# Two layers of masked cross-attention on one core: maxima of the scores taken from ScalarE's copies in SBUF instead of from PSUM

## The chip, the cores and the metric

The kernel runs on one NeuronCore of a Trainium2 chip. The metric is the device time of one execution in microseconds (us): 3316.82, the median of three runs (3314.22 to 3318.01). All data is 32-bit floating point. TensorE multiplies matrices from SBUF into PSUM; VectorE, ScalarE and GpSimd work on elements; the sequencer of SyncE (SP) issues most DMAs. GpSimd is called POOL in the profile, VectorE DVE, ScalarE ACT, TensorE PE.

## The reference

Two attention layers follow one another on x (4 batches, 512 rows, 320 columns) with one context (4 batches, 1024 tokens of 512). Both have 20 heads of 16 columns. Cut to what matters:

```python
# layer 0: text = tokens 0..1019, ip = the last 4
q, k_t, v_t = x @ W_q, text @ W_k, text @ W_v              # split into heads
probs_t = softmax(q k_t^T / 4)                              # 1020 tokens
text_out = probs_t v_t
qsem = l2norm(probs_t @ text)                               # 512 columns per head and row
fused = q k_ip^T / 4 + 0.5 * qsem l2norm(ip)^T
ip_out = (softmax(fused) * spatial_mask) v_ip
x = (text_out + ip_out) @ W_out + b_out + x
# layer 1: text = tokens 0..76, ip = the other 947
out = softmax(q k^T / 4) v + softmax(q k_ip^T / 4) v_ip     # two softmaxes, own maxima
x = out @ Wo^T + bo + x
```

The product `probs_t @ text` (each head's probabilities with all 512 context columns) is the bulk of the arithmetic.

## The kernel before

**Passes.** A turn is 128 rows of one batch (16 turns); it has five groups of four heads, so there are 80 passes (`gi`), one for each turn and group. Scores lie with the tokens on partitions: a fill (`fill`, L547) computes, for four heads and half of the 1024 tokens, 16 products of 128 tokens by 128 rows into two PSUM tiles `sc` (two heads each, 1024 columns). ScalarE copies each into SBUF (`e`, 128 x 1024). Maxima over the tokens go the way that matters here: in `fill`, VectorE reduces each PSUM tile over its four token tiles into `m` (a half is `c`; for layer 0 the two halves are joined by `m<-m`); then a transpose of 32x32 blocks and a reduce to `zz` (`fold0`, L941), a transpose of `zz` on TensorE (`turn_tops`, L572, tile `mx`), a reduce to `zt` (`spread`, L578), a DMA to DRAM and one back as a broadcast, `bc`. `do_exp` then adds `bc` (minus the maximum) to `e` on VectorE and takes the exponent on ScalarE, in place; for the half `c == 0` GpSimd also subtracts one head's block from another (L964).

**Units.** A pass is two units of two heads (`Unit`, L1002). A unit multiplies exponents with the context by seven block products in place of eight (Strassen's scheme), 8 matmul records each: `part0` has products 11 and 21 of blocks, `part1` t1 and t2, `part2` 22 and t3, `part3` t4. They accumulate in three PSUM banks b1, b2, b3. GpSimd forms sums of exponents for them: `sum2` (tile `s`, L1032), L1051 and L1053. ScalarE copies the first product as `p1` and a later state of b1 as `u`; the state of b3 after t1 is copied by VectorE as `p5`, whose last 21 columns (the window that carries the values) have `p1` subtracted at once (L1064 and L1065). VectorE adds pairs of these (tile `c`) and ScalarE squares the sums; the 21 columns go to `pv`.

**Order.** `mm` (L77) keeps TensorE's instructions in program order, and `vec` (L90) does so for VectorE. ScalarE's and GpSimd's instructions are ordered by the tile framework's planner, which goes by its own costs; at run time every engine works through its queue in order. After each part, `stop(gi, k)` (L1262, k = 0 to 7 over the two units) issues other work: layer 0's next fill at k = 0 (first half) and k = 2 (second half), layer 1's fill at k = 4 and 6 (`visit`, L1241), its adds and exponents (`do_adds`), the exponents of the next pass (queue `ew`, one item at k = 1, one inside `part2` of the first unit, two at k = 6), projections of the next batch (queue `proj`), and what ends a turn (`after`, `late`, `norm`). `fold0` comes at k = 3. `part0` of the second unit and `part2` of the first issue the transposes of `zz` behind their products, and then what `between` returns: `ask`, the reduce to `zt` with the DMAs.

**Layer 1's two maxima.** In layer 1 tokens 0 to 76 and the others have separate maxima. The first token tile holds both, so the reduce of the first half leaves it out (`lo`), and `mask` (L626) joins it later as (e + cut) max m, where `cut[:, 1:2]` holds -1e30 on the first 77 partitions and 0 elsewhere; `x` is the copy with the opposite mask (L620).

`p1`, `p5`, `m` and `x` have one buffer each; `e` has eight for layer 0 and six for layer 1.

Of the kernel before, what the change touches and what calls it, by code (L numbers as in the profile page):

```python
# [15 lines left out]
ALU = mybir.AluOpType  # L16
AX = mybir.AxisListType
# [3 lines left out]
P = 128  # L21
# [24 lines left out]
EH = E // 2  # L46
WIN = EH + V0W
TH = TT // 2
# [8 lines left out]
def xattn_pair(ctx_stack: ExitStack, tc: tile.TileContext, a: dict, out: bass.AP):  # L57
    nc = tc.nc
# [18 lines left out]
    def mm(out, lhsT, rhs, start, stop, on=False):  # L77
        tc.keep_in_program_order(nc.tensor.matmul(out, lhsT=lhsT, rhs=rhs, start=start, stop=stop, skip_group_check=on))  # L78
# [11 lines left out]
    vec = InOrder(nc.vector)  # L90
# [46 lines left out]
    mask = cst.tile([P, TT + 1], F32, name="mask")  # L137
    last = cst.tile([P, 2], F32, name="last")
    cut = cst.tile([P, 2], F32, name="cut")
# [384 lines left out]
    after = deque()  # L524
    ew = deque()
    bits = deque()

    def gap(n=1):
        for _ in range(n):
            if bits:  # L530
                bits.popleft()()
# [15 lines left out]
    def fill(l, k, c, m, pl, tag, name):  # L547

        ps = [ps_sc.tile([P, 2, 512], F32, tag="sc", name=f"sc{name}_{c}_{i}") for i in range(2)]
        n = D + 1 - l  # L550
        for j in range(TH):
            t = (TH * c + j) * P
            for r in range(4):
                mm(ps[r // 2][:, r % 2, j * P : (j + 1) * P], kq[l][k][32 * r : 32 * r + n, t : t + P],
                   qq[l][k][32 * r : 32 * r + n, :], True, True)
        e = [pl.tile([P, 2, TH, P], F32, tag=tag, name=f"e{name}_{c}_{i}") for i in range(2)]


        lo = l * (1 - c)
        for i in range(2):  # L560
            nc.scalar.copy(e[i].rearrange("p h t s -> p (h t s)"), ps[i].rearrange("p h n -> p (h n)"))  # L561
            j = 1 - i
            vec.tensor_reduce(m[:, c, 2 * j : 2 * j + 2, :],
                              ps[j][:, :, lo * P : TH * P].rearrange("p h (t s) -> p h s t", s=P), AX.X, ALU.max)
        if c and not l:
            vec.tensor_tensor(m[:, 0], m[:, 0], m[:, 1], ALU.max)
        return e
# [10 lines left out]
    def spread(pt, rows, tag, name):  # L578

        n = rows * P // ZW  # L580
        zt = st2.tile([ZW, ZW], F32, tag="zt", name=f"zt{name}")
        vec.tensor_reduce(zt[:n, :], pt[:n, 0:P].rearrange("r (b j) -> r j b", j=ZW), AX.X, ALU.max, negate=True)
        zd = dr.tile([rows, P], F32, tag=tag, name=f"{tag}{name}")
        nc.sync.dma_start(zd.rearrange("h (k j) -> (h k) j", j=ZW), zt[:n, :])
        return zd
# [15 lines left out]
    def load_values(z, turn, g):  # L601
        v = st2.tile([P, TT + 1, V1Q], F32, tag="v1q", name=f"v1q_{turn}_{g}")
        nc.sync.dma_start(v, z.v1d[:, :, g * 4 * V1W : g * 4 * V1W + V1Q])
        return v

    class Once:
# [6 lines left out]
        def fill(self, c):  # L613
# [8 lines left out]
            if c:  # L622
                free.append(self.k)
                load_next()

        def mask(self):  # L626

            for i in range(2):
                x = self.m[:, 0, 2 * i : 2 * i + 2, :]
                vec.scalar_tensor_tensor(x, self.e[0][i][:, :, 0, :], cut[:, 1:2], x, ALU.add, ALU.max)  # L630

        def top(self, k):

# [25 lines left out]
        def ask(self, pt):  # L659

            zd = spread(pt, 8, "zd1", self.name)
            self.bc = bc = big.tile([P, 2, 4, P], F32, tag="bc1", name=f"bc{self.name}")
            keep(nc.sync.dma_start(bc[:NTXT1, 0], zd[0:4, :].partition_broadcast(NTXT1)))
            keep(nc.sync.dma_start(bc[NTXT1:, 0], zd[4:8, :].partition_broadcast(P - NTXT1)))
            keep(nc.sync.dma_start(bc[:, 1], zd[4:8, :].partition_broadcast(P)))
            self.v = load_values(self.z, self.turn, self.g)
# [22 lines left out]
    now = {"fill": None, "fold": None, "add": []}  # L689

    def load_next():
        if waiting and free:
            q = waiting.popleft()
            q.load(free.popleft())
            loaded.append((q, stops[0]))

    def begin(*where):
        now["fill"] = loaded.popleft()[0] if loaded and stops[0] >= loaded[0][1] + 2 else None
        if now["fill"]:
            now["fill"].where = where  # L700

    def do_fill(c):
        if now["fill"]:
            now["fill"].fill(c)

    def do_mask():
        if now["fill"]:
            now["fill"].mask()

    def do_fold(all=False):  # L710
        q = now["fill"]
# [6 lines left out]
    def do_rest():  # L718
        if now["fold"]:
            now["fold"].fold_rest()  # L720
# [281 lines left out]
    class Unit:  # L1002
# [43 lines left out]
        def part0(self, between):  # L1046
            self.b1, self.b2 = self.psum(0)[:, 0:WIN], self.psum(1)[:, 0:WIN]
            self.product(self.b1, "11", "11", True)
            self.p1 = big.tile([P, WIN], F32, tag="p1", name=f"p1_{self.name}")
            nc.scalar.copy(self.p1, self.b1)  # L1050
            nc.gpsimd.tensor_tensor(self.e("11"), self.e("11"), self.s2, ALU.add)  # L1051
            self.product(self.b2, "12", "21", True)
            nc.gpsimd.tensor_tensor(self.e("12"), self.e("12"), self.s2, ALU.subtract)  # L1053
            ask = between and between()
            self.add_square(self.b2[:, 0:EH], self.p1[:, 0:EH], 0, 0)
            vec.tensor_tensor(self.values(0), self.b2[:, EH:], self.p1[:, EH:], ALU.add)
            if ask:
                ask()

        def part1(self):  # L1060
            self.b3 = self.psum(2)[:, 0:WIN]
            self.product(self.b3, "11", "t1", True)
            self.p5 = big.tile([P, WIN], F32, tag="p5", name=f"p5_{self.name}")
            vec.tensor_copy(self.p5[:, 0:EH], self.b3[:, 0:EH])  # L1064
            vec.tensor_tensor(self.p5[:, EH:], self.b3[:, EH:], self.p1[:, EH:], ALU.subtract)  # L1065
            self.product(self.b1[:, 0:EH], "s2", "t2", False)
            self.u = big.tile([P, EH], F32, tag="u", name=f"u_{self.name}")
            nc.scalar.copy(self.u, self.b1[:, 0:EH])

        def part2(self, between):  # L1070
            self.product(self.b3[:, 0:EH], "12", "22", False)
            ask = between and between()
            self.add_square(self.b3[:, 0:EH], self.u, 0, 1)
            if ask:
                ask()
            if not self.i:
                item(ew)
            self.product(self.b1[:, 0:EH], "21", "t3", False)
            self.add_square(self.b1[:, 0:EH], self.p5[:, 0:EH], 1, 1)

        def part3(self):
            self.product(self.b1, "22", "t4", False)
            self.square(self.b1[:, 0:EH], 1, 0)
            vec.tensor_tensor(self.values(1), self.b1[:, EH:], self.p5[:, EH:], ALU.add)

    def finish(turn):
# [137 lines left out]
    for g in range(HG):  # L1224
        for r in range(4):
            c = 64 * g + D * r
# [8 lines left out]
    def item(*queues):  # L1235
        for q in queues:
            if q:
                q.popleft()()
                break

    def visit(gi, k):  # L1241

        if gi == len(G) - 1:
            if k == 0:
                begin(ep, "e0")
            if k == 4:
                begin(e1p, "e1")
            if k == 6:
                do_values()
                do_adds(2)  # L1250
            do_fill(k // 2 % 2)
            return
        if k < 4:
            fill0(gi + 1, k // 2)
        if k == 4:
            begin(e1p, "e1")
            do_fill(0)
        if k == 6:
            do_values()
            do_fill(1)  # L1260

    def stop(gi, k):  # L1262

        end = gi == len(G) - 1
        if k == 1:
            do_mask() if end else do_rest()
            item(ew)
        if k == 3:
            do_fold(True) if end else fold0(gi + 1)
        if k == 6:  # L1270
            item(ew)
            item(ew)
        if k == 7 and not end:
            do_fold(gi + 1 == len(G) - 1)
        if k == 7 and end and now["fill"]:
            now["fold"] = now["fill"]
            now["fill"] = None
            bits.extend(now["fold"].pieces())
        if k < 3:
            item(after, late, *([proj] if k else []))  # L1280
        elif k % 2:
            item(late, proj)
        do_adds(({3: 4, 7: 2} if end else {3: 1, 5: 3}).get(k, 0))
        if k == 3:
            item(norm)
        if k == 5:
            do_mask()
        if k % 2 == 0:
            visit(gi, k)
        stops[0] += 1  # L1290

    units = {}
# [7 lines left out]
    for gi, (turn, g) in enumerate(G):  # L1300
        b, s = TURNS[turn]
# [7 lines left out]
        for i in range(2):  # L1309
            u = units.pop((gi, i))  # L1310
            end = gi == len(G) - 1
# [20 lines left out]
    while late:  # L1332
        if now["fold"] and not bits:
            ask = do_maxima()
# [4 lines left out]
    ask = do_maxima()  # L1339
# [36 lines left out]
```

## Time and profile before

| | |
|---|---|
| median of three runs | 3316.82 us |
| profiled execution | 3314.02 us, of which the span of instructions is 3312.3 us |
| mean granted TensorE clock | 0.985 |
| busy: PE / PEld / DVE / ACT / POOL | 3208.6 / 2594.7 / 2506.2 / 1855.7 / 1043.7 us |
| VectorE's reduces of `sc` (620) | 706.9 us |
| VectorE's adds of `bc` to `e` (770) | 803.5 us |
| ScalarE's copies of `sc` (620) | 614.5 us |
| VectorE's copies of `p5` (160) | 66.7 us |

Busy time is the union of the instructions of an engine. A group's line in the profile shows count, busy time, mean duration of one in ns, the idle time of the engine just before them, and what ended it. A matmul in 32-bit precision stands as two records. Since an add has two tile names on the right (`e<-e,bc`), a step can be found by its tiles although helpers give it one line, L88.

### The profile page before, as it was taken

The numbers are of one execution on the slowest core, as the hardware profiler recorded it, in microseconds if no ns is written. First come the engines' busy times: TensorE is split into PE (matmuls) and PEld (weight loads), VectorE is DVE, ScalarE is ACT, GpSimd is POOL, SyncE is SP. The second block draws the span as 40 slices with busy tenths as digits, with TensorE's granted clock in tenths as the row PEclk, the third lists the DMA queues.
The fourth block names the chain that finished last, engine by engine and source line by source line (L and its number), as shares of the span: only waits on it lengthen the run. The fifth ranks groups of instructions, "written<-read, shape, count | busy, mean of one in ns | idle before, by whom it ended". The sixth has DMA issues, their size and how long they took to land.

```text
span 3312.3 us, 72573 instructions
## 1 busy us (share of the span) xinstructions
PE 3208.6 (97%) x27740; PEld 2594.7 (78%) x27740; DVE 2506.2 (76%) x4172; ACT 1855.7 (56%) x3373; POOL 1043.7 (32%) x1123
## 2 busy tenths in 40 slices
PE   7999999999999999999999999999999999999988
PEld 5777888878788788887878888887787778787765
DVE  3344577788877777778887787778898888889874
ACT  1333455566555555566655555566666656666643
POOL 3333223323332332323333232323333333333320
PEclk9999999999999999999999999999999999999987
DMA  6433344333444344332344434333233233232221
GB/s 213 112 79 97 96 117 96 92 71 65 102 99 125 92 119 118 75 79 65 68 101 127 121 90 109 97 72 70 58 86 89 63 67 69 59 72 62 64 54 39
DMA packets 648147, 293.89 MB, mean 89 GB/s; under 512 B 491530, under 2 KB 602282, under 8 KB 647802
## 3 DMA queue, kind: packets, MB, share of 16 engines
q1 hardware_dynamic: 646762, 285.65, 36.1%
q8 instruction: 221, 3.62, 0.5%
q0 software_dynamic: 864, 3.41, 0.4%
q14 instruction: 124, 1.02, 0.1%
q10 hardware_dynamic: 176, 0.20, 0.0%
HBM read 248.43 MB, written 40.47 MB: 87 GB/s over the span
## 4 chain that ended last, share of the span: by engine, by line
PE 80%; DVE 10%; DMA 5%; ACT 3%; issue 2%; SPq 1%; POOL 0%; DVEq 0%; POOLq 0%; ACTq 0%
PE b L78 52%; PE sc L78 9%; PE pt_v L78 4%; PE pv L78 4%; PE pt_k L78 4%; DVE e L88 4%; DMA bc<-zd 2%; PE pt_q L78 2%; DVE m L88 2%; PE pt_y L78 2%; DMA zd<-zt 1%; ACT e L561 1%; ACT e L675 1%; DVE x L88 1%; PE mx L78 1%
## 5 line engine op out<-in xcount | busy, mean ns | idle before, releaser
L88 DVE TENSOR_REDUCE m<-sc 128x256 f32<-128x1024 f32 (+1 forms) x620 | 706.9, 1156 | 240.9 <-PE sc L78 166.7
L88 DVE TENSOR_TENSOR e<-e,bc 128x1024 f32<-128x1024 f32 (+2 forms) x770 | 803.5, 1082 | 21.6 <-DMA bc<-zd 21.1
L78 PE MATMUL b<-xv_t,e 128*128 128x277 f32 x2560 | 686.2, 410 | 7.9 <-DVE c L88 7.8
L561 ACT COPY e<-sc 128x1024 f32<-128x1024 f32 x620 | 614.5, 1006 | 82.8 <-DVE m L88 34.2
L78 PE MATMUL b<-xv,e 128*128 128x277 f32 x2560 | 631.3, 398 | 9.2 <-ACT e L962 9.2
L78 PEld LDWEIGHTS b<-xv,e 128*128 128x128 f32 x2560 | 483.4, 190 | 130.6 <-ACT e L962 11.4
L964 POOL TENSOR_TENSOR e<-e 128x512 f32<-128x512 f32 x160 | 230.6, 1441 | 1114.0 <-ACT e L962 1114.0
L78 PEld LDWEIGHTS b<-xv_t,e 128*128 128x128 f32 x2560 | 460.7, 190 | 134.8 <-DVE c L88 11.8
L962 ACT ACTIVATE e<-e 128x1024 f32<-128x1024 f32 x320 | 338.5, 1058 | 225.4 <-DVE e L88 224.6
L675 ACT ACTIVATE e<-e 128x1024 f32<-128x1024 f32 x300 | 316.1, 1058 | 194.3 <-DVE e L88 185.8
L78 PEld LDWEIGHTS sc<-qq,kq 17*128 17x128 f32 (+1 forms) x9920 | 307.1, 186 | 89.9 <-issue 85.0
L78 PE MATMUL sc<-qq,kq 17*128 17x128 f32 (+1 forms) x9920 | 366.8, 283 | 2.1 <-DMA kq<-kd 1.5
L1036 ACT ACTIVATE junk<-c 128x256 f32<-128x256 f32 x480 | 197.6, 412 | 287.8 <-DVE c L88 281.0
L78 PE MATMUL b<-xs,e 128*128 128x256 f32 x1280 | 313.5, 389 | 36.2 <-DVE p L88 27.5
L1051 POOL TENSOR_TENSOR e<-e,s 128x512 f32<-128x512 f32 x160 | 208.4, 1302 | 420.1 <-PE b L78 419.4
L78 PE MATMUL b<-xs_t,e 128*128 128x256 f32 x1280 | 307.3, 384 | 0.0
L78 PEld LDWEIGHTS b<-xs,e 128*128 128x128 f32 x1280 | 241.6, 193 | 81.1 <-issue 47.1
L78 PE MATMUL b<-xs_t,s 128*128 128x256 f32 x1280 | 302.3, 379 | 0.0
L88 DVE TENSOR_TENSOR c<-b,p 128x256 f32<-128x256 f32 x320 | 132.9, 415 | 222.7 <-PE b L78 166.2
L78 PEld LDWEIGHTS b<-xs_t,s 128*128 128x128 f32 x1280 | 242.7, 190 | 39.6
L78 PEld LDWEIGHTS b<-xs_t,e 128*128 128x128 f32 x1280 | 241.8, 194 | 36.9 <-issue 1.0
L1032 POOL TENSOR_TENSOR s<-e,e 128x512 f32<-128x512 f32 x160 | 203.1, 1270 | 122.6 <-ACT e L962 101.5
(213 smaller groups left out, 3439.3 us busy)
## 6 DMA issues: line engine op xcount, KB each, us to landing
kq<-kd SPq DMA_DIRECT2D x632, 64.0 KB
bc<-zd SPq DMA_DIRECT2D x155, 256.0 KB
v1q<-v1d SPq DMA_DIRECT2D x80, 373.5 KB
xv<-v0d SPq DMA_DIRECT2D x320, 42.0 KB
xv_t<-v0d SPq DMA_DIRECT2D x320, 42.0 KB
bc<-zd SPq DMA_DIRECT2D x75, 154.0 KB
L_xattn_W_k<-in_L_xattn_W_k_dram SPq DMA_DIRECT2D x13, 640.0 KB
L_xattn_Wv_ip<-in_L_xattn_Wv_ip_dram SPq DMA_DIRECT2D x13, 640.0 KB
```

The source lines that it names most:

```text
L78: tc.keep_in_program_order(nc.tensor.matmul(out, lhsT=lhsT, rhs=rhs, start=start, stop=stop, skip_group_check=on))
L88: return lambda *args, **kw: keep(getattr(self.engine, name)(*args, **kw))
L561: nc.scalar.copy(e[i].rearrange("p h t s -> p (h t s)"), ps[i].rearrange("p h n -> p (h n)"))
L675: nc.scalar.activation(flat, flat, AF.Exp)
L962: nc.scalar.activation(flat, flat, AF.Exp)
L964: nc.gpsimd.tensor_tensor(e[:, 1], e[:, 1], e[:, 0], ALU.subtract)
L1032: nc.gpsimd.tensor_tensor(self.s2, self.e("21"), self.e("22"), ALU.add)
L1036: nc.scalar.activation(junk, x, AF.Square, accum_out=self.w["ss"][:, self.h + r, k : k + 1])
L1051: nc.gpsimd.tensor_tensor(self.e("11"), self.e("11"), self.s2, ALU.add)
```

## The change

Four things change.

- In `fill` the reduces from PSUM are gone. Behind ScalarE's two copies VectorE takes pairwise maxima of the copies: two steps of 512 columns for the first half of layer 0; four of 512 for every second half, which take in `m` twice; for the first half of layer 1 two masked steps of 256 columns ((e0 + cut) max e1) and two plain ones (e2 max e3). `mask` and its calls go.
- `p5` is copied whole (277 columns) by ScalarE; the subtraction of `p1` from its last 21 columns moves into `part3`, from SBUF to SBUF.
- A queue `mid` is emptied inside `fill`, between the copies and the maxima (or after `visit`, where no fill took place). Into it go `part0`'s first sums (`first_sums`), the `ew` item of the first unit's `part2`, and the second of the two at k = 6.
- In `part0`, `ask` is issued before the first sums instead of behind them.

```diff
+    mid = deque()
...
         e = [pl.tile([P, 2, TH, P], F32, tag=tag, name=f"e{name}_{c}_{i}") for i in range(2)]
-        lo = l * (1 - c)
         for i in range(2):
             nc.scalar.copy(e[i].rearrange("p h t s -> p (h t s)"), ps[i].rearrange("p h n -> p (h n)"))
-            j = 1 - i
-            vec.tensor_reduce(m[:, c, 2 * j : 2 * j + 2, :],
-                              ps[j][:, :, lo * P : TH * P].rearrange("p h (t s) -> p h s t", s=P), AX.X, ALU.max)
+        while mid:
+            mid.popleft()()
+        for i in range(2):
+            top, tiles = m[:, :, 2 * i : 2 * i + 2, :], e[i].rearrange("p h t s -> p t h s")
+            if c:
+                vec.tensor_tensor(top, top, tiles[:, 0:2], ALU.max)
+                vec.tensor_tensor(top, top, tiles[:, 2:4], ALU.max)
+            elif l:
+                vec.scalar_tensor_tensor(top[:, 0], tiles[:, 0], cut[:, 1:2], tiles[:, 1], ALU.add, ALU.max)
+                vec.tensor_tensor(top[:, 1], tiles[:, 2], tiles[:, 3], ALU.max)
+            else:
+                vec.tensor_tensor(top, tiles[:, 0:2], tiles[:, 2:4], ALU.max)
         if c and not l:
             vec.tensor_tensor(m[:, 0], m[:, 0], m[:, 1], ALU.max)
...
-        def mask(self):
-            for i in range(2):
-                x = self.m[:, 0, 2 * i : 2 * i + 2, :]
-                vec.scalar_tensor_tensor(x, self.e[0][i][:, :, 0, :], cut[:, 1:2], x, ALU.add, ALU.max)
...
             ask = between and between()
+            if ask:
+                ask()
+            mid.append(self.first_sums)
+
+        def first_sums(self):
             self.add_square(self.b2[:, 0:EH], self.p1[:, 0:EH], 0, 0)
             vec.tensor_tensor(self.values(0), self.b2[:, EH:], self.p1[:, EH:], ALU.add)
-            if ask:
-                ask()
...
             self.p5 = big.tile([P, WIN], F32, tag="p5", name=f"p5_{self.name}")
-            vec.tensor_copy(self.p5[:, 0:EH], self.b3[:, 0:EH])
-            vec.tensor_tensor(self.p5[:, EH:], self.b3[:, EH:], self.p1[:, EH:], ALU.subtract)
+            nc.scalar.copy(self.p5, self.b3)
...
-            if not self.i:
-                item(ew)
+            if not self.i and ew:
+                mid.append(ew.popleft())
...
             self.square(self.b1[:, 0:EH], 1, 0)
+            vec.tensor_tensor(self.p5[:, EH:], self.p5[:, EH:], self.p1[:, EH:], ALU.subtract)
             vec.tensor_tensor(self.values(1), self.b1[:, EH:], self.p5[:, EH:], ALU.add)
...
         if k == 1:
-            do_mask() if end else do_rest()
+            do_rest()
             item(ew)
...
         if k == 6:
             item(ew)
-            item(ew)
+            if ew:
+                mid.append(ew.popleft())
...
-        if k == 5:
-            do_mask()
         if k % 2 == 0:
             visit(gi, k)
+            while mid:
+                mid.popleft()()
```

More of the change, by code (lines that the diff above doesn't have):

```diff
@@ L704, in do_fill @@
             now["fill"].fill(c)
-    def do_mask():
-        if now["fill"]:
-            now["fill"].mask()
     def do_fold(all=False):
```

## The prediction

> **What bounds the kernel now.** I read the page's busy line first, then busy time in stretches of 100 us, then TensorE's waits, then the timeline of one pass, and last the groups by shape for prices.
>
> ```profile
> PE 3208.6 (97%) x27740; PEld 2594.7 (78%) x27740; DVE 2506.2 (76%) x4172; ACT 1855.7 (56%) x3373; POOL 1043.7 (32%) x1123
> ```
>
> TensorE is busy 97% of the span. In the stretches (length, busy PE, PEld, DVE, ACT, POOL, granted clock, DMA share, GB/s) there are two kinds:
>
> ```profile
> 1000.00:1100.00 100.00, 99.77 (x802) 80.79 (x801) 74.83 (x125) 58.95 (x103) 29.56 (x38) 1.00 0.48 125
> ...
> 2600.00:2700.00 100.00, 98.09 (x845) 79.37 (x844) 89.21 (x151) 60.96 (x111) 36.87 (x34) 0.98 0.31 67
> ```
>
> Where projections of the next batch are interleaved (the first), TensorE is full and VectorE has a quarter to spare; where there are none (the second: about 700 to 900, 1500 to 1700, 2300 to 2500, 2500 to 3150 us; "tight" below) VectorE is busy too. TensorE's waits between 100 and 3150 us:
>
> ```profile
> PE b L78 <- DVE p L88: 23.4, 19, 2.3
> PE b L78 <- issue: 8.7, 3, 2.9
> PE b L78 <- DVE c L88: 7.8, 14, 0.6
> PE b L78 <- ACT e L962: 6.4, 3, 2.7
> ```
>
> The columns are total us, times, longest. TensorE is idle 49.3 us of these 3050, so this is nearly all that can be won there, and 23.4 of it ends with VectorE's copy of p5 (the 8.7 "issue" stand at the same place: three ends of a turn). A gap of 1.9 us or more is followed some 11 us later by 3.4 us at half clock in most cases, which costs 1.7 us more. What could be lost shows in the timeline of a tight pass (start, us, engine, line, operation):
>
> ```profile
> 2898.71 1.17 PE L78 MATMUL sc<-qq,kq 17*128 17x128 f32 x32
> ...
> 2900.02 1.27 POOL L1032 TENSOR_TENSOR s<-e,e 128x512 f32<-128x512 f32 x1
> 2900.03 2.41 DVE L88 TENSOR_REDUCE m<-sc 128x256 f32<-128x1024 f32 x2 [0.79 <-PE sc L78]
> ...
> 2900.19 0.99 ACT L561 COPY e<-sc 128x1024 f32<-128x1024 f32 x1
> ...
> 2901.34 1.01 ACT L561 COPY e<-sc 128x1024 f32<-128x1024 f32 x1 [0.16 <-POOL s L1032]
> ...
> 2902.47 0.69 DVE L88 TENSOR_TENSOR m<-m 128x512 f32<-128x512 f32 x1
> ...
> 2903.19 0.71 DVE L88 STREAM_TRANSPOSE m<-m 128x512 f32<-128x512 f32 x1
> ...
> 2903.94 0.69 DVE L88 TENSOR_REDUCE zz<-m 128x16 f32<-128x512 f32 x1
> ...
> 2905.53 0.27 PE L93 MATMUL mx<-ident,zz 128*128 128x128 f32 x1
> ```
>
> After the second half of a fill (sc, ends 2899.88) VectorE reduces, joins the halves (m<-m), transposes, reduces to zz, ends 2904.63; TensorE comes to the transpose of zz (mx) at 2905.53. So the chain takes 4.75 us and TensorE allows 5.65. I measured this interval for all 80 passes: the chain takes 4.7 in nearly all; TensorE allows 5.65 in 30, 6.09 in 11, 7.3 or more in the rest, apart from the first pass.
>
> Prices (busy us, mean ns):
>
> ```profile
> L88 DVE TENSOR_REDUCE m<-sc 128x256 f32<-128x1024 f32 x470 | 564.2, 1222 | 206.8 <-PE sc L78 150.8 <-ACT e L561 52.5
> ...
> L88 DVE TENSOR_TENSOR x<-m 128x512 f32<-128x512 f32 x75 | 73.1, 974 | 2.5
> ...
> L88 DVE TENSOR_TENSOR m<-m 128x512 f32<-128x512 f32 x80 | 55.4, 692 | 2.7
> ```
>
> ```profile
> L1032 POOL TENSOR_TENSOR s<-e,e 128x512 f32<-128x512 f32 x160 | 203.1, 1270 | 122.6 <-ACT e L962 101.5 <-PE sc L78 11.6 <-ACT junk L1036 0.4
> ```
>
> **The change part by part.** The profiled execution took 3314.0 us, 2.8 below the median of 3316.8; the sum starts from 3314.0.
>
> *Busy time of VectorE.* Gone: 470 reduces of 1024 columns (564 us), 150 of 768 (143), 150 mask steps (66), the p5 copies (67). Added: 780 steps of 512 columns at 691 ns (539), 150 masked and 150 plain steps of 256 columns at 0.48 and 0.41 (134). That is 167 us less. It is worth time only where TensorE waits for VectorE.
>
> *The chain from sc to zz.* This sets my forecast. A step of 512 took 691 to 693 ns whenever GpSimd was not running an add (the m<-m row). After the change: ScalarE starts its first copy 0.12 us after sc and takes 1.0; the first maximum starts at 1.20. Four steps of 0.69, two of which read what the step before wrote (such pairs stood 0.03 apart, independent ones overlapped by 0.08), end at 3.94; m<-m at 4.66; from its end to the end of zz took 1.47, and the subtraction of p5's 21 columns, now queued there, adds 0.09: 6.22. mx then starts at about 6.28 instead of 5.65. Price: 0.63 us in 30 passes and 0.19 in 11, 21 us. Behind the waiting maxima on VectorE stand m<-m, the transpose, zz and then layer 1's adds; mx waits for zz, and ScalarE's next exponents for the adds. The exponent's add put in front (1.22 us) starts before sc ends and is over by 0.6, so it is covered by the copy; were it late, it would add up to 1.2.
>
> *GpSimd in that chain.* The reduces read PSUM: 319 of the 470 large ones overlapped a GpSimd add and took 1223 ns, the others 1217. Steps with two SBUF inputs don't: x<-m took 692 alone and 1421 where it overlapped one, and its row's mean of 974 is this mixture; GpSimd's adds go from 1.27 to 2.0. The exponent's ScalarE step, if ScalarE takes steps as the program issues them, now follows both copies (0.12 + 2.0 + 1.06 = 3.2 us after sc), and GpSimd's sum s (L1032) waits for just this; today it runs in the reduces' shadow. So it asks for the port amid the maxima (1.2 to 4.66). Does it get in between? At 1543.41 an add on GpSimd asked while VectorE ran a row of such adds; it ended 1.47 later, so after the running one, and VectorE's next add took 1.89 instead of 1.22. So I charge 1.27 less the 0.1 by which starts overlap, 1.15: the wait at mx becomes 1.78 us in 30 passes and 1.34 in 11, together 68 us. Without any collision it is 21; 68 is the likelier end, by that row.
>
> [...]
>
> *p5 on ScalarE.* 160 copies of 277 columns at 0.39 us (L1050's row). In the first half of a pass ScalarE has only the two copies of sc and a square in front: they end about 2.6 us after sc, p5 at 3.0, and TensorE needs it at 3.6: free. In the second half (layer 1's fill) two masked copies x of 0.51 and the squares stand there as well. Today ScalarE starts the copies of sc 0.9 to 1.0 late in tight passes, because an exponent waits for VectorE; 0.9 + 2.0 + 1.0 + 0.4 = 4.3 against 3.55. I charge 0.75 in 30 passes, 22 us; the bounds are 0 (p5 planned ahead of the x) and 1.7 (VectorE's adds come 0.9 later, behind the longer chain). This takes the place of 8 us of today's p5 waits outside ends of turns.
>
> *Ends of turns.* Nine tight ones hold 22.5 us of waits. There ScalarE's copies stand behind an exponent that waits for a row of small VectorE steps. p5 would come 0.4 earlier (two copies and 0.39 against reduces, 0.41 and 0.17), but layer 1's maxima, at the end of the same queue, can make that row up to 1.8 later. I take 0, bounds -4 and +16.
>
> *First sums behind the fill, the ask before them.* The sums (0.42 and 0.17) fill the wait for the first copy; their squares on ScalarE are in the p5 sum above. The ask's DMAs on SP's queue go out 0.6 earlier, and no wait for them binds today: 0. p1 stays in use until the subtraction, so the next unit's p1 copy starts up to 1 us later; the product that needs its bank comes more than 3 us after, so 0, and about 1 a pass if that cover goes. Moving the exponent's add behind the third sum frees that sum: the 7.8 us of "DVE c" go.
>
> *Later GpSimd adds, exponents, clock.* Block 11's add (L1051) must be ready at the first product after the fill; by the same collisions it comes 1.0 later and has 1.5 to spare (2922.72 against 2924.21): 0, bound 20. Three batch ends with "ACT e" may lose 2 each. Waits of 1.78 lie just below the 1.9 that half clock followed; bound 50 if they pass it.
>
> Sum: 68 + 22 - 8 - 8 = 74. 3314 + 74 = 3388; with the 2.8 by which the median lies above the profiled execution, 3391.
>
> **The rivals.** *Collision rarely binds* (GpSimd's sum comes before or after the maxima): 21 + 22 - 16 = 27, less where p5 goes first: 3323 to 3355. For it: s may be planned elsewhere; against: any moment in a stretch of 3.4 us collides.
>
> *Faster.* VectorE's relief decides: the waits for p5 (23.4 + 8.7), for c (7.8) and half of some 17 us of half clock go, 48 us, and the chain costs nothing: 3266, or up to 3307 where half of it is lost at mx. For it: VectorE is what TensorE waits for today, and loses 167 us of 2506. Against: these waits are latency at two places. It decides from the point where zz ends within 5.6 us of sc.
>
> *No difference.* The chain costs 21 and the p5 and c waits saved pay for it (32 + 8, of which half at ends of turns stays): 3310 to 3323.
>
> **How the numbers follow.** Chances: forecast 0.52 (3355 to 3440), collision rarely binds 0.25, no difference 0.08, faster 0.15. The range leaves out most of the faster case and the upper bounds of p5, the clock and GpSimd together: 3308 to 3440. About 0.2% (6.6 us) is what a measurement of this kernel can tell from no change: faster 0.15, same 0.07, slower 0.78.
>
> **What would show it.** Right: a wait "PE mx <- DVE zz" of 0.6 to 1.8 us, some 40 times, where there are three now; sc to zz at 6.2 to 7.4 us; steps m<-e with a mean well above 691; "PE b <- ACT p" in second halves; VectorE's busy time below 2506 but less so than by 167. Wrong: no wait at mx, or zz within 5.7 us of sc; a p5 that never binds; maxima at 691 on average, which would mean that GpSimd stays out of the way.

## The result: 3716 us, 12% slower

The changed kernel took 3716.12 us (median of five, 3710.87 to 3723.04) against 3316.82 before: a ratio of 1.120, 95% interval 1.118 to 1.122. The direction was forecast, the size was not: 400 us in place of 74. The profiled execution took 3720.5 us, span 3718.6, mean granted clock 0.939 (0.985 before).

The page's busy line; VectorE did lose work, but only 16 us in place of 167:

```profile
PE 3368.5 (91%) x27740; PEld 2693.7 (72%) x27740; DVE 2490.3 (67%) x4322; ACT 1871.1 (50%) x3533; POOL 1027.6 (28%) x1123
```

TensorE's waits between 100 and 3550 us (total us, times, longest):

```profile
PE mx L93 <- DVE zz L88: 163.0, 41, 5.3
PE b L78 <- ACT p L1066: 49.6, 41, 3.2
PE mx L93 <- DVE xr L88: 30.5, 15, 2.3
PE b L78 <- issue: 14.9, 4, 4.2
```

The wait that the prediction named is there, in 41 places, but with 4.0 us each in place of 1.3 to 1.8. The third row is new too: at 15 ends of turns `mx` comes only after `xr`, VectorE's next step behind `zz`. The timeline of a tight pass, one with the longest wait, shows where its 5.3 us come from (start, us, engine, line, operation, and in brackets the idle time before it with what ended it):

```profile
3059.34 1.17 PE L78 MATMUL sc<-qq,kq 17*128 17x128 f32 x32
...
3059.78 2.10 DVE L88 TENSOR_TENSOR e<-e,bc 128x1024 f32<-128x1024 f32 x1
...
3061.92 1.06 ACT L961 ACTIVATE e<-e 128x1024 f32<-128x1024 f32 x1 [1.45 <-DVE e L88]
...
3062.89 1.91 ACT L561 COPY e<-sc 128x1024 f32<-128x1024 f32 x2
3063.12 1.27 POOL L1031 TENSOR_TENSOR s<-e,e 128x512 f32<-128x512 f32 x1 [2.32 <-ACT e L961]
...
3063.91 5.09 DVE L88 TENSOR_TENSOR m<-m,e 128x512 f32<-128x512 f32 x4 [2.02 <-ACT e L561]
...
3064.60 1.47 POOL L1050 TENSOR_TENSOR e<-e,s 128x512 f32<-128x512 f32 x1 [0.21 <-PE b L78]
...
3066.41 1.33 POOL L1052 TENSOR_TENSOR e<-e,s 128x512 f32<-128x512 f32 x1 [0.34 <-PE b L78]
...
3070.76 0.69 DVE L88 TENSOR_REDUCE zz<-m 128x16 f32<-128x512 f32 x1
...
3071.59 0.44 PE L93 MATMUL mx<-ident,zz 128*128 128x128 f32 x1 [5.27 <-DVE zz L88]
```

The scores end at 3060.51. The exponent of the moved `ew` add (L961) stands ahead of the copies on ScalarE, and it waits for that add, which itself meets a GpSimd step (2.10 us in place of 1.22). So the copies start 2.38 us after the scores, not 0.12, and the first maximum at 3.40, not 1.20. Then three GpSimd adds (L1031, L1050, L1052) run beside the four maxima, not one: they took 1.03, 1.64, 1.74 and 0.69, 5.09 in all against 2.75. `zz` ends 10.94 us after the scores; forecast were 6.2 to 7.4. Of the 30 passes in which TensorE allowed 5.65 us before, 15 end `zz` at this time; in 14 others, where the copies start 1.5 to 2.1 us after the scores, it ends at 10.1 to 10.7.

What collisions cost over the whole run is in the groups by shape (mean ns behind the busy time); the forecast's uncollided price was 691:

```profile
L88 DVE TENSOR_TENSOR m<-m,e 128x512 f32<-128x512 f32 x620 | 536.3, 885 | 353.8 <-ACT e L561 343.1
...
L88 DVE TENSOR_TENSOR p<-p,p 128x21 f32<-128x21 f32 x160 | 73.4, 459 | 0.0
```

And half clock comes with the wait. The ten us from the end of the wait above (length, busy PE, PEld, DVE, ACT, POOL, granted clock, DMA share, GB/s) had a granted clock of 0.68, where the ten from 3060 had 1.00:

```profile
3071.00:3081.00 10.00, 9.41 (x57) 7.69 (x58) 8.27 (x18) 6.04 (x11) 0.80 (x3) 0.68 0.14 31
```

**Two sums that hold for all kernels here.** Span less busy PE is TensorE's idle time (before 103.7 us, after 350.1); (1 - granted clock) x span estimates the time lost to half clock (before 50, after 227). The two grew by 246 + 177 = 423 us, against 406 in the span. (TensorE's busy time for the same 27740 matmul records grew by 160 us, which is near the 177.) For every run below their differences from before add up to within 25 us of the difference in span, so they are given with each as "idle" and "clock".

### The profile page after: what moved, and what is told of

Read it like the earlier page. It is cut to its first block, busy times and chain, and to the rows that moved or that the text cites. A ratio compares the mean times of both kernels' runs of the same rounds, so it can differ in the third digit from the quotient of the medians.

```text
span 3718.6 us, 73128 instructions
## 1 busy us (share of the span) xinstructions
PE 3368.5 (91%) x27740; PEld 2693.7 (72%) x27740; DVE 2490.3 (67%) x4322; ACT 1871.1 (50%) x3533; POOL 1027.6 (28%) x1123
## 3 DMA queue, kind: packets, MB, share of 16 engines
q0 software_dynamic: 864, 3.41, 0.3%
## 4 chain that ended last, share of the span: by engine, by line
PE 65%; DVE 20%; ACT 7%; issue 5%; DMA 2%; POOL 1%; SPq 0%; DVEq 0%; ACTq 0%; POOLq 0%
PE b L78 42%; DVE m L88 10%; PE sc L78 8%; ACT e L561 4%; PE pt_k L78 4%; PE pv L78 4%; DVE e L88 4%; PE pt_v L78 3%; PE pt_q L78 1%; DVE zz L88 1%; DVE p L88 1%; ACT e L961 1%; PE mx L93 1%; PE pt_y L78 1%; DVE x L88 1%
## 5 line engine op out<-in xcount | busy, mean ns | idle before, releaser
L78 PE MATMUL b<-xv_t,e 128*128 128x277 f32 x2560 | 769.7, 448 | 16.8 <-POOL e L1050 9.4
L88 DVE TENSOR_TENSOR e<-e,bc 128x1024 f32<-128x1024 f32 (+2 forms) x770 | 783.5, 1058 | 2.1 <-DMA bc<-zd 2.1
L88 DVE TENSOR_TENSOR m<-m,e 128x512 f32<-128x512 f32 x620 | 536.3, 885 | 353.8 <-ACT e L561 343.1
L78 PEld LDWEIGHTS b<-xv_t,e 128*128 128x128 f32 x2560 | 511.2, 210 | 171.3 <-POOL e L1050 10.7
L561 ACT COPY e<-sc 128x1024 f32<-128x1024 f32 x620 | 592.6, 1007 | 16.2 <-PE sc L78 12.6
L963 POOL TENSOR_TENSOR e<-e 128x512 f32<-128x512 f32 x160 | 205.3, 1283 | 1226.7 <-ACT e L961 1226.7
L961 ACT ACTIVATE e<-e 128x1024 f32<-128x1024 f32 x320 | 338.0, 1057 | 278.5 <-DVE e L88 278.2
L78 PE MATMUL sc<-qq,kq 17*128 17x128 f32 (+1 forms) x9920 | 401.0, 302 | 2.3 <-DMA kq<-kd 1.5
L78 PEld LDWEIGHTS sc<-qq,kq 17*128 17x128 f32 (+1 forms) x9920 | 337.0, 203 | 83.0 <-issue 75.2
L1050 POOL TENSOR_TENSOR e<-e,s 128x512 f32<-128x512 f32 x160 | 232.2, 1451 | 350.2 <-PE b L78 349.9
L1049 ACT COPY p<-b 128x277 f32<-128x277 f32 x160 | 62.5, 391 | 451.3 <-DVE p L88 309.9
L1031 POOL TENSOR_TENSOR s<-e,e 128x512 f32<-128x512 f32 x160 | 203.2, 1270 | 256.4 <-ACT e L961 250.5
```

The costliest lines, as they stand in the source:

```text
L88: return lambda *args, **kw: keep(getattr(self.engine, name)(*args, **kw))
L961: nc.scalar.activation(flat, flat, AF.Exp)
L963: nc.gpsimd.tensor_tensor(e[:, 1], e[:, 1], e[:, 0], ALU.subtract)
L1031: nc.gpsimd.tensor_tensor(self.s2, self.e("21"), self.e("22"), ALU.add)
```

## Experiments

"zz" is the time from the end of the scores to the end of `zz`, as it comes most often in the 30 tightest passes (those in which TensorE allowed 5.65 us before): 4.74 us before, 10.94 after. Where a kernel has two common values, both are given or the share of the passes. Ratios are to the kernel before, with 95% intervals. "Port", in the prediction and in the expectations, is my name for whatever stretches a VectorE step with two SBUF inputs beside a GpSimd add: before, the 29 `x<-m` that overlapped an add took 1421 ns in the mean, the other 46 took 692. These times are what the traces show; no run shows what lies behind them.

### The parts one by one

**The maxima alone**

```diff
 in fill, against the kernel after:
-        while mid:
-            mid.popleft()()
 first sums, ew items and p5 as before
```

> Only the maxima are changed: pairwise maxima of the copies with the mask in the first step; p5 stays on VectorE, and the first sums and the ew add keep their old places (the ew add behind the third sum, ahead of the fill, so its exponent has left ScalarE before the scores are done). If the loss of the whole change comes from ScalarE's exponent standing ahead of the copies (theory A), zz should end 7 to 8 us after the scores here instead of 10.1 to 10.9, and the time should be near 3450. If it comes from the three GpSimd adds that share VectorE's port (theory B), zz should still end 9 us or more after the scores and the time should be 3550 or above. If the maxima are only as dear as the prediction had it (68 us), the time is near 3385.

3471.6 us, 1.046 (1.042 to 1.049); zz 7.38; idle +78, clock +58. The chain of a tight pass:

```profile
2743.20 1.90 ACT L560 COPY e<-sc 128x1024 f32<-128x1024 f32 x2
...
2744.22 2.75 DVE L88 TENSOR_TENSOR m<-m,e 128x512 f32<-128x512 f32 x4 [2.08 <-ACT e L560]
...
2746.83 1.27 POOL L1047 TENSOR_TENSOR e<-e,s 128x512 f32<-128x512 f32 x1 [2.52 <-PE b L78]
2747.01 1.64 DVE L88 TENSOR_TENSOR m<-m 128x512 f32<-128x512 f32 x1
...
2750.26 0.30 PE L93 MATMUL mx<-ident,zz 128*128 128x128 f32 x1 [1.71 <-DVE zz L88]
```

The time is nearest to the first of the three expectations. The length is that of the forecast's chain (four undisturbed maxima, 2.75 us, one collision of 0.95, zz 7.4), and TensorE's waits at `mx` sum to 56.4 us in 35 places, near the forecast's 68. But the collision is another one: it hits `m<-m`, and the add it meets is L1047 (in 28 of the 30 tight passes), while the sum s (L1028 here), which the forecast had in mind, starts 0.1 to 0.6 us after the scores and is over when the maxima have hardly begun. Nor does it come everywhere: in the 11 passes where TensorE allowed 6.09 us no step is stretched, zz ends at 6.0 to 6.3, and the waits are 0.6 us where 14.7 were forecast. And the kernel lost 152: waits for VectorE's p5 rose, over the whole run, from 27.5 to 49.2 us, since p5's copy stands behind the longer maxima in VectorE's queue, and the clock took 58.

**p5 alone**

```diff
-            vec.tensor_copy(self.p5[:, 0:EH], self.b3[:, 0:EH])
-            vec.tensor_tensor(self.p5[:, EH:], self.b3[:, EH:], self.p1[:, EH:], ALU.subtract)
+            nc.scalar.copy(self.p5, self.b3)
 and in part3, ahead of the second sum:
+            vec.tensor_tensor(self.p5[:, EH:], self.p5[:, EH:], self.p1[:, EH:], ALU.subtract)
```

> Only p5 is changed: ScalarE copies it whole, VectorE subtracts p1 just ahead of the second sum. If p5 is a large part of the loss (theory D: the waits of TensorE for ScalarE's p copy, 49.6 us in the changed kernel, and the half clock they bring), the time is 3360 to 3400. If those waits are only there because the copies and exponents are shifted by the maxima, the time is 3300 to 3335. The prediction's own term for this part is 22 - 8 = +14, less what VectorE is relieved of: about 3325.

3313.5 us, 0.9987 (0.9971 to 1.0003): no difference that can be told; zz 4.99, idle +3, clock -3. By itself this part is innocent.

**Both**

```diff
 the maxima alone, and p5 alone's edit
```

> The changed kernel with both moved steps at their old places: the pairwise maxima and the p5 copy on ScalarE remain. Nothing is left out. The maxima alone took 3471.6 and p5 alone took 5 us off; if the parts add, 3455 to 3480. The 49 us that TensorE waited for VectorE's p copy behind the maxima should turn into a shorter wait for ScalarE's copy: below 3450 if that copy is free by then, above 3480 if it stands behind copies and exponents on ScalarE.

3560.7 us, 1.072 (1.069 to 1.075), 89 more than the maxima alone: the parts do not add. idle +130, clock +100, zz 9.13 in half of the tight passes, 7.62 in most others. The time is above 3480, as expected for a late p5 copy, but that is not the reason: TensorE's waits for p5 are shorter than with the maxima alone (43.8 against 49.2 us), and those at `mx` rose from 56.4 to 100.4. The lines of a pass with 9.13:

```profile
2810.22 1.64 DVE L88 TENSOR_TENSOR m<-m 128x512 f32<-128x512 f32 x1
2811.41 1.57 POOL L1049 TENSOR_TENSOR e<-e,s 128x512 f32<-128x512 f32 x1
...
2811.79 1.24 DVE L88 TENSOR_TENSOR p<-p,p 128x21 f32<-128x21 f32 x1
...
2814.79 0.30 PE L93 MATMUL mx<-ident,zz 128*128 128x128 f32 x1 [3.46 <-DVE zz L88]
```

The subtraction, 21 columns and 0.17 us alone, reads SBUF twice and stands between the maxima and `zz`. Where it meets the next GpSimd add it takes 1.24 us. With p5 alone the chain ended sooner and it was not in the way.

**Both, without the moved subtraction**

```diff
+            nc.scalar.copy(self.p5[:, 0:EH], self.b3[:, 0:EH])
+            vec.tensor_tensor(self.p5[:, EH:], self.b3[:, EH:], self.p1[:, EH:], ALU.subtract)
 both in part1, the copy on ScalarE now of the first 256 of the 277 columns only
```

> The maxima, with p5 split between the engines: ScalarE copies its first half, VectorE subtracts p1 from the second half at once, reading PSUM, so that no subtraction of p5 is left beside the second sum. First sums and ew add at their old places; nothing is left out. If the 89 us that p5 on ScalarE cost on top of the maxima came from the moved subtraction (1.24 us in place of 0.17 in the chain that ends in zz, where it meets GpSimd's add), the time is 3440 to 3480 and zz ends at 7.4 again in the passes that had 9.1. If they came from ScalarE's order (copies that start 0.6 to 0.9 us late), it stays at 3530 or above.

3444.6 us, 1.038 (1.035 to 1.040), zz 7.38 again; idle +76, clock +36. All 89 us of the p5 move, counted from the maxima alone, are gone, and 27 more. The second collision in the chain went with the subtraction. The copy on ScalarE is a little shorter too (256 columns took 0.37 us in the kernel with the split alone, further below; the changed kernel's 277 took 0.39); where the 27 come from is not shown beyond TensorE's waits for p5 (41.8 against 49.2 us) and the clock (36 against 58).

**The moved steps**

```diff
 the kernel after, ew item as before:
-            if not self.i and ew:
-                mid.append(ew.popleft())
+            if not self.i:
+                item(ew)
```

> The changed kernel with the ew add at its old place (behind the third sum, ahead of the fill) and only the first sums left between copies and maxima. Nothing is left out. If the moved ew add carries the loss of the order (by its exponent ahead of the copies and its own 1.2 to 2.1 us on VectorE), zz ends 7.4 to 8 us after the scores and the time is 3450 to 3500, as with the maxima alone. If the first sums carry it, it stays above 3600.

```diff
 the kernel after, first sums as before (in part0, ahead of the fill), ew item still in mid
```

> The changed kernel with the first sums at their old place and only the ew add left between copies and maxima. Nothing is left out. The counterpart: if the moved ew add carries the loss of the order the time stays at 3650 to 3720, if the first sums carry it, it falls to 3450 to 3500.

With the ew add back: 3575.3 us, 1.077 (1.075 to 1.079); zz 9.13 in half of the tight passes; idle +146, clock +97. With the sums back: 3704.9 us, 1.116 (1.115 to 1.118); zz 10.94; idle +238, clock +169. Both answers agree: the ew add costs 141 or 144 us on top of maxima and p5, the sums 11 to 15. So the steps from before to after are +152, +89, +15 and +141 in this order. They add up because each is counted from the one before; another order would share the loss out differently, and only the first is what its part costs alone. The expectation of 3450 to 3500 for the first of these kernels failed: it left out the 89 that p5 adds to the maxima.

**The order alone, maxima from PSUM**

```diff
 the kernel before, with mid as in the change; in fill:
         for i in range(2):
             nc.scalar.copy(...)
+        while mid:
+            mid.popleft()()
+        for i in range(2):
             j = 1 - i
             vec.tensor_reduce(...)
```

> Only the order is changed: the first sums and the ew item are issued behind the fill's copies and ahead of its maxima, which stay reductions from PSUM with the mask at its old place. If the moved ew add brings its exponent ahead of the copies (theory A), the copies should start over 2 us after the scores, but the reductions do not read the copies: zz should end about 2 to 2.5 us later than the 4.7 us of before only through the moved VectorE steps (an add of 1.2 to 2.1 us and the sums), i.e. 6 to 7 us after the scores, around the 5.65 to 6.09 that TensorE allows: 3317 to 3360. If the order is innocent, zz stays below 5.6 us and the time is 3305 to 3325.

3773.3 us, 1.136 (1.133 to 1.139), zz 9.17, where at most 3360 and 7 were expected. This kernel is not the clean test it was meant to be:

```profile
3073.71 1.91 ACT L562 COPY e<-sc 128x1024 f32<-128x1024 f32 x2
...
3075.65 1.23 DVE L88 TENSOR_REDUCE m<-sc 128x256 f32<-128x1024 f32 x1 [2.94 <-ACT e L562]
```

Issued behind both copies, the first reduce waits for the second copy's end (3075.62), although it reads PSUM, as the copy does. It takes the tile that is copied second, and in this program the two engines read one PSUM tile only one after the other: 0.03 us lie between them here, and in the kernel before no copy overlapped the reduce of the same tile, in 620 pairs, with 0.03 us between them at the least. Before, copies and reduces alternated over the two tiles and shared this time. So it has the late copies and, on top, no overlap. It does show that the late exponent needs no change of the maxima: copies start 1.9 us after the scores here too. (idle +288, clock +169.)

### Late copies or the port

**Copies kept ahead of the exponent**

```diff
-            nc.scalar.copy(e[i]...)
+            keep(nc.scalar.copy(e[i]...))
-            nc.scalar.activation(flat, flat, AF.Exp)
+            keep(nc.scalar.activation(flat, flat, AF.Exp))
```

> The changed kernel with one more constraint: on ScalarE the copies of a fill and layer 0's exponents keep the order in which they are written, so that the exponent of the moved ew add comes behind both copies. Nothing is left out. If the late copies (theory A) are the main part, the copies start 0.1 us after the scores again, zz ends 8 to 9 us after them, and the time falls to 3580 to 3620. If the moved VectorE add and sums ahead of the maxima, and the port, are the main part, the maxima still start no earlier than the add's end plus the sums, zz stays near 9.5 to 10 and the time is 3660 to 3720.

3661.6 us, 1.103 (1.101 to 1.105): 55 less than after, less than I expected of the late copies: the time is that of the other branch, 3660 to 3720. They start 0.11 us after the scores now, but zz still ends at 9.41. In one tight pass (the scores ended at 2765.95):

```profile
2767.11 3.79 DVE L88 TENSOR_TENSOR m<-m,e 128x512 f32<-128x512 f32 x4 [0.67 <-ACT e L561]
...
2770.93 1.64 DVE L88 TENSOR_TENSOR m<-m 128x512 f32<-128x512 f32 x1
...
2772.50 1.24 DVE L88 TENSOR_TENSOR p<-p,p 128x21 f32<-128x21 f32 x1
```

The chain starts 2.2 us earlier and gives 0.7 back, since it now meets all three adds in full: the last maximum (1.75), `m<-m` (1.64) and the subtraction (1.24), 3.1 us of waiting against 2.3 after. (idle +199, clock +140.)

**One operand from PSUM**

```diff
+            raw = ps[i].rearrange("p h (t s) -> p t h s", s=P)
-                vec.tensor_tensor(top, top, tiles[:, 0:2], ALU.max)
+                vec.tensor_tensor(top, top, raw[:, 0:2], ALU.max)
 and so in every maximum of the fill
```

> The changed kernel with one operand of each pairwise maximum read from the scores in PSUM in place of the copy in SBUF; everything else as in the changed kernel. If GpSimd's adds on the shared port are a large part of the loss (theory B), maxima that waited 1.6 to 1.7 us go back to about 0.7 and zz comes 2.3 us earlier, 7.8 to 8.6 us after the scores: 3560 to 3610. If the late copies (theory A) are the main part and the port is not, zz stays at 9.5 us or more and the time is 3660 or above.

3584.7 us, 1.080 (1.077 to 1.084), 131 less than after, as the first expectation had it. The maxima's group:

```profile
L88 DVE TENSOR_TENSOR m<-m,sc 128x512 f32<-128x512 f32 x620 | 412.3, 685 | 352.8 <-ACT e L561 342.2
```

685 ns in the mean, 885 after: with one operand in PSUM the mean of these maxima is no longer than that of undisturbed ones (691). The copies are as late as ever, and zz ends at 9.42 or 7.68, depending on whether `m<-m`, still with two SBUF operands, meets an add. (idle +161, clock +94.)

**The same without the other parts, and with the copies first**

```diff
 the maxima alone, one operand from PSUM
```

> The kernel of the maxima alone (first sums, ew add and p5 at their old places) with one operand of each maximum read from PSUM in place of the copy. Nothing is left out. In the kernel with the maxima alone the four maxima are not stretched; it is the next step, the maximum of the two halves (0.69 us alone, 1.65 to 1.80 there), that meets GpSimd's add, and it still reads both operands from SBUF. If the shared port is only a matter of which steps meet GpSimd's adds, this changes little: zz at 7.3 to 7.5 us, 3440 to 3480. If a maximum with an operand in PSUM is faster or lets GpSimd's adds run earlier, zz falls to 6.3 or less and the time is 3330 to 3400.

```diff
 the kernel after, copies first and one operand from PSUM
```

> The changed kernel with both mends: ScalarE's copies kept ahead of the moved exponent, and one operand of each maximum from PSUM. Each alone took 55 and 131 us off 3716. If lateness and port add up, 3520 to 3540 with zz at 7.4 to 8.4 us. If with the copies on time the collisions only move to the two later steps (the maximum of the halves and the subtraction of p5, which still read SBUF twice), zz stays at 8.3 to 8.5 and the time is 3570 to 3620.

The first: 3418.3 us, 1.030 (1.027 to 1.032), 53 less than the maxima alone; zz 6.25 in some tight passes, 7.38 in others, where `m<-m` took 1.66. That is between the two expectations: the undisturbed maxima are not faster with an operand in PSUM (685 ns in the row above, 691 before), but GpSimd's adds shifted and missed `m<-m` in part of the passes. (idle +58, clock +22.) The second: 3487.1 us, 1.051 (1.048 to 1.053), 229 less than after, more than 55 + 131 and below both expectations: zz 7.74, with `m<-m` at 1.04 and the subtraction at 1.24 the only steps left to collide. (idle +97, clock +55.)

**Without two of the three adds**

```diff
-            nc.gpsimd.tensor_tensor(self.e("11"), self.e("11"), self.s2, ALU.add)
+            nc.gpsimd.tensor_tensor(self.e("11")[:, :, 0:2], self.e("11")[:, :, 0:2], self.s2[:, :, 0:2], ALU.add)
 and so for "12"
```

> The changed kernel, leaving out most of GpSimd's two adds behind the s add (products 11 and 12: 8 of 512 columns are done, so the products that use them are wrong; TensorE's work is the same). If meeting these adds on the shared port is what stretches the maxima, the maximum of the halves and the subtraction of p5, the chain keeps only its late copies and the first, shorter meeting: zz at 8.4 to 8.9 us in the tight passes in place of 10.9, and 3520 to 3580. If the steps are slow for another reason (VectorE's own queue, semaphores), they stay at 1.6 to 1.75 us and the time stays above 3650.

> The same with ScalarE's copies kept ahead of the moved exponent; again most of the two adds is left out. With both suspects gone, only the length of the chain is left (copy before maximum, four maxima, the maximum of the halves, the subtraction, the second sum, transpose, last maximum): zz at 6.3 to 6.5 us against the 5.65 to 6.09 that TensorE allows, 3350 to 3400. If it stays above 3450, something other than lateness and port is at work.

With late copies: 3523.3 us, 1.062 (1.059 to 1.064), zz 8.7 in 14 of the 30 tight passes and 8.1 in 11, as expected or less:

```profile
2912.91 3.08 DVE L88 TENSOR_TENSOR m<-m,e 128x512 f32<-128x512 f32 x4 [2.02 <-ACT e L561]
...
2913.83 0.21 POOL L1050 TENSOR_TENSOR e<-e,s 128x8 f32<-128x8 f32 x1 [0.45 <-PE b L78]
...
2916.03 0.69 DVE L88 TENSOR_TENSOR m<-m 128x512 f32<-128x512 f32 x1
```

The maxima took 1.02, 0.69, 0.69 and 0.69, then `m<-m` 0.69 and the subtraction 0.17. So to take these two adds away was worth 193 of the 400 us (idle +121, clock +77); of these, at most 9.4 are TensorE's own waits for L1050 in the changed kernel. With the copies first: 3469.9 us, 1.046 (1.044 to 1.048), zz 7.40, where 3350 to 3400 was expected; above 3450, the expectation said, something else would be at work. The lines show the same collision: the third add, s, had been left whole, and moved into the way:

```profile
2771.74 3.80 DVE L88 TENSOR_TENSOR m<-m,e 128x512 f32<-128x512 f32 x4 [1.58 <-ACT e L561]
...
2773.72 1.27 POOL L1031 TENSOR_TENSOR s<-e,e 128x512 f32<-128x512 f32 x1 [2.26 <-ACT e L961]
```

The fourth maximum, from 2773.79, took 1.75. Without that 1.06, zz would end 6.34 us after the scores, near the forecast's uncollided 6.22; this is worked out, since no run took all three adds away. (idle +89, clock +37.)

### Is anything of the change worth keeping?

**p5 split, maxima as before**

```diff
 the kernel before, p5 split as above
```

> The kernel before with p5 split in the same way: first half copied by ScalarE, second half subtracted by VectorE from PSUM at once. The maxima stay as before; nothing is left out. TensorE waits 23 us for VectorE's p steps before, of which the copy is 0.41 us in each second half. If the two halves of p5 end side by side, 5 to 15 us go: 3303 to 3314. If ScalarE's half comes behind the copies and the masks, as the whole copy did, it is within 0.2% of before.

**p5 on ScalarE, mask copies later**

```diff
 p5 alone, and layer 1's x (two masked copies on ScalarE) moved from fill(0) into mask()
```

> The kernel with p5 alone on ScalarE, and layer 1's two mask copies (x) issued with the mask step of VectorE instead of inside the fill, so that p5's copy no longer stands behind one of them. Nothing is left out. p5 alone waited 30 us in 27 places, 1.1 to 1.6 us each; 0.5 us of each is a mask copy: about 13 us less, 3300 to 3308, 0.3 to 0.5% below before. If the planner puts something else (an exponent) in the place of the mask copy, it stays at 3310 to 3320.

The split: 3338.4 us, 1.0055 (1.0037 to 1.0073), slower by half a per cent, against both expectations. VectorE's subtraction reads the PSUM tile that ScalarE copies, and waits for it:

```profile
2785.99 0.37 ACT L1064 COPY p<-b 128x256 f32<-128x256 f32 x1
...
2786.40 0.18 DVE L88 TENSOR_TENSOR p<-b,p 128x21 f32<-128x21 f32 x1 [0.76 <-ACT p L1064]
```

TensorE's waits for p5 rose, over the whole run, from 27.5 to 43.2 us (idle +22, clock 0). The second: 3313.4 us, 0.9988 (0.9974 to 1.0003), no better than p5 alone; waits for the p copy fell by 3.4 us, not 13 (idle -2, clock -10). No version run here beats the kernel before by more than 0.2%.

## Why the prediction was right and wrong

**Right: what decides, and the direction.** The chain from sc to zz became what TensorE waits for, in about 40 places. The uncollided chain (6.22 forecast, 0.09 of it for the subtraction) ended at 6.1 in 8 of the 11 passes of the maxima alone that met no add, and a chain with one collision (7.4) at 7.38 there; the 68 us at `mx` were 56.4. That this sum came close is partly luck: the add that collided was L1047 and not s, it came in 28 passes and not in 41, and the moved `ew` add, from which the forecast had derived the collision, was not in that kernel. The collision with GpSimd's adds was the right thing to weigh, and all three other cases (collision rarely binds, faster, no difference) are out.

**Wrong first: the order of ScalarE.** The step that failed is "if ScalarE takes steps as the program issues them". I used it to place the exponent behind both copies, and treated the moved add as "covered by the copy; were it late, it would add up to 1.2". The planner put the exponent first, and exponent plus add made the first maximum 2.2 us late in half of the tight passes and 1.3 to 2.0 in most others. The add was not over at 0.6 us after the scores either, but at 1.38, since it met a GpSimd step itself (2.10 us). The text of the kernel says that the planner orders ScalarE by its own costs; a bound for the other order (the add's 1.22 or 2.10 and the exponent's 1.06 ahead of the copies) could have been worked out from the rows of before. Taken by itself this step is the smaller part: with the order mended and all else as changed, 55 of the 400 us came back.

**Wrong second: one collision in place of three.** I priced one add, 1.15 us, on the argument that s asks amid the maxima. Once the chain is longer, L1050 and L1052 fall into it as well, and without these two adds 193 us came back, more than from any other single edit here. The profile before showed them beside a step with two SBUF inputs: of the 29 `x<-m` that overlapped an add (1421 ns in the mean), 26 met L1051 and 3 met L1053, the same two adds under their old line numbers:

```profile
2921.45 1.26 POOL L1051 TENSOR_TENSOR e<-e,s 128x512 f32<-128x512 f32 x1 [1.41 <-PE b L78]
...
2921.61 1.66 DVE L88 TENSOR_TENSOR x<-m 128x512 f32<-128x512 f32 x1
```

In the tight pass above the excess is 2.34 us. Put together, 7.37 forecast + 2.20 for the late start + 1.19 for the further collisions + 0.16 for the steps behind the maxima = 10.92, against 10.94 measured. The two are not independent: with the copies on time the collisions cost 3.1, which is why that repair gave back only 55 us.

**Wrong third: half clock at nothing.** I took waits of 1.78 us to "lie just below the 1.9" that half clock followed, and bounded it at 50. By the estimate above it cost 177 us here, and 58 even in the kernel with the maxima alone, whose waits at `mx` (1.71 us) are of just this size. The reading of the profile before was thin. Between 100 and 3150 us it has 12 waits of 1.9 us or more; behind 7 of them a stretch at half clock begins, and it begins within 1.2 us of the wait's end, not some 11 us later. No wait there lies between 1.5 and 1.9 us, so nothing showed that such a wait is free.

**Mis-sized: ends of turns and p5.** Ends of turns were put at 0 with a bound of +16. The waits ahead of the product behind p5 in first halves, the large ones at such ends, rose from 23.8 to 53.2 us, and 30.5 us at `mx` behind `xr` came new, as the same late chain with one more step; there the chain is 9.5 us too. In second halves, where I charged 22, the waits were 10.2 in 15 places (12.4 in 8 before). The moved subtraction was to add 0.09 us to the chain; with p5 alone zz came 0.25 later and cost no time, but with the maxima the subtraction took up to 1.24 us in the chain: with p5's move 89 us. One slip weighs nothing: 1.27 less 0.1 is 1.17 and not 1.15.

**Busy time of VectorE.** Forecast -167, measured -16: 620 maxima at 885 instead of 691 ns are 120 us, and 160 subtractions at 459 instead of 171 ns another 46.

**Open.** Why the planner takes the exponent first is not visible in a profile. That half clock follows the waits is read from the records; no run held the waits and changed only the clock. No run mends the order and takes all three adds away, so what the longer chain costs without either is an estimate.

## What to carry to other kernels

Price a chain that is about to become the latest one with every step of the other engine that can fall into its new, longer length, not with the one that falls into it today (here three GpSimd adds in place of one); a collision cost the small step as much as the large one here (0.17 us became 1.24, and 0.69 became 1.64 or 1.75). Where a planner orders an engine's queue, a step moved ahead of a fill can bring its consumer along (here the copies started 2.38 us after the scores in place of 0.12): price both orders, and expect parts that cost nothing alone to cost much once another part has used up the slack (p5's move: nothing alone, 89 us on top of the maxima). Try a maximum with one operand from PSUM: here it took 685 ns in the mean, with both in SBUF 885; reducing from PSUM beside the copy, as the kernel did, hardly felt it (1223 ns beside a GpSimd add, 1217 otherwise).

## What the runs showed of the hardware

- **Half clock after shorter gaps than the prediction took.** With the maxima alone, 16 of 24 TensorE gaps of 1.6 to 1.8 us (between 400 and 3200 us) were followed within 2.1 us by the start of a stretch at half clock, 3.41 us long in 13 cases and 6.83 in three; of 40 gaps of 0.4 to 1.6 us, 1 was.
- **A collision cost 21 columns about as much as 512.** 512 columns went from 0.69 to 1.64 or 1.75 us, 21 columns from 0.17 to 1.24: about 1 us either way, most of a GpSimd add of 1.27. A step that met only the end of an add lost less (the first maximum of the changed kernel, 1.03 us).
- **Two engines on one PSUM tile.** VectorE's reads started 0.03 and 0.04 us after the end of ScalarE's in the two kernels shown above (a reduce after 2.94 us of idling, a subtraction after 0.76). The profile puts both waits down to ScalarE's copy, and splitting the reading of one tile over two engines made the kernel half a per cent slower.
